# Summing the exponentials of some head pairs on GpSimd before they reach TensorE

## The chip, the core and the metric

The kernel runs on one core of a Trainium2 chip. A core has five engines with instruction queues of their own: PE (TensorE, matrix products, into PSUM), DVE (VectorE, elementwise work), ACT (ScalarE, activation functions and copies), POOL (GpSimd, general cores that also do elementwise work on SBUF) and SP (SyncE, which here issues most DMAs). Each queue is worked through in order, and engines wait for each other by semaphores. The metric is the device time of one execution in microseconds (us). Times of instructions come from one profiled execution.

## What is computed

Two attention layers stand one behind the other, on eight images of 512 channels and 32x32 = 1024 positions. The first is the one that is touched. After a group normalization and the projections it rounds q, k and v to 8 bits over their whole range, and then does plain attention over 8 heads of 64 channels:

```
q, k, v = fake_quant(q), fake_quant(k), fake_quant(v)
w = einsum('bct,bcs->bts', q * scale, k * scale)
w = softmax(w, axis=-1)
a = einsum('bts,bcs->bct', w, v)
x = x + einsum('oc,bct->bot', proj_w, a) + proj_b
```

The softmax needs, for each query, the sum of the exponentials over all 1024 keys. The second layer is single-head attention over 512 channels, with its own normalization and projections, and a residual. All of it is fp32.

## The kernel before

**Stages.** A first stage projects q, k and v of all images and stores them in DRAM, together with their extremes. From then on two streams run through each other: the first layer's attention, and for the image before it the rest (the first layer's output projection, and all of the second layer, whose products are cut up in Strassen's manner into seven, `seven()`).

**Units of the attention.** `attention()` (line 999) walks over 8 images b, 4 pairs of heads j, 2 halves hf of 512 queries, and 8 tiles s of 128 keys: 512 units u, 16 a pair. In a unit `scores(u)` makes two products into a PSUM tile st (128 keys, 2 heads x 512 queries), and ACT writes the exponentials to the fp32 tile pt, 128x1024. There are four slots for pt; the exponential of unit u+4 writes where unit u's was. `split(u)` makes two fp16 parts of pt, in the tile two: a cast, and what the cast left out, a subtraction on DVE. The cast runs on ACT, but for s = 2 and 6 of images 1 to 7 on GpSimd (line 1079). `over_keys` multiplies both parts with v, into av. `totals` sums over keys: both parts times a block of ones, four products a unit, each into its own 32 rows of the PSUM tile sm, over the eight units of a half.

**An iteration** takes four units (lines 1193 to 1237): two scores, then the products with v and the sums of units u to u+3, the splits of two units, two more scores, and after the second iteration of a half `finish`, which copies av and sm out of PSUM on ACT. So scores run six to ten units ahead. Where little other work stands between iterations (`dense`) or after the projection (`late`) the order within an iteration differs.

**The sums' way out.** After the second half, `finish` sends the rows of sums by two small DMAs to a tile apart that has them spread over 128 partitions; there DVE adds the two parts and takes the reciprocal, which goes to DRAM (rs_d) and comes back broadcast over the channels by two DMAs into rs. Later one DVE operation (`divide`) multiplies ao by it.

**Loads.** `load_pair(b, j, u)` (line 942) is called one pair ahead. It fetches raw q, k and v, 128x1024 fp32 each, through a pool of two slots (`raw_p`): q and k at once, and v when q's slot is free. Each takes two DVE passes (`quant`, `quant2`).

**The order.** The second part of the program is planned as it is written: the class `InOrder` keeps a time estimate for DVE, ACT and PE. `do(cost, work, ready)` advances an engine's clock and issues; `later(name, cost, work, ready, within)` puts a chore off, and `fill` issues chores where they fit before the next urgent operation; `settle(name)` issues the rest of a kind. The estimates only set the order of the instructions in the queues; on the chip each instruction waits for its data. GpSimd has no such clock: its instructions stand in program order. Besides the casts and, in the first image, some casts that are done by DMA, it computes the power -1/2 in the group normalizations (line 263).

Of the kernel before, what the change touches and what calls it, by code (L numbers as in the profile page):

```python
# [18 lines left out]
P = 128  # L19
# [39 lines left out]
def attn_pair_kernel(  # L59
# [95 lines left out]
    dve, act, pe = InOrder(nc.vector), InOrder(nc.scalar), InOrder(nc.tensor)  # L155

# [71 lines left out]
    def norm_steps(  # L228
# [22 lines left out]
        def offsets():  # L251
# [11 lines left out]
        nc.gpsimd.tensor_tensor(rstd, rstd, mhalf[:, 0:n], ALU.pow)  # L263
        dve.do(
            0.15, lambda: dve.tensor_mul(rstd, rstd, vec[:, wcol + c0 : wcol + c0 + n]), dve.t + 1.4
# [41 lines left out]
    with ExitStack() as fast:  # L307
# [633 lines left out]

        def load_pair(b, j, u=None):

            nm = f"{b}_{j}"
            raws = []

            def fetch(i, src):
                if (b, j, i) == (0, 0, 2):
                    raw = aop.tile([P, NH, 512], F32, tag="ao", name="raw_first").rearrange(
                        "p h n -> p (h n)"  # L950
                    )
                else:
                    raw = raw_p.tile([P, T], F32, tag="raw", name=f"raw_{nm}_{i}")
# [9 lines left out]
            fetch(1, k_d[b][j])  # L963
# [8 lines left out]
            def quants(i):  # L972
                for n, step in enumerate((quant, quant2, *([whole] if i == 2 and b == 0 else []))):
                    name, work = "qk" if i < 2 else "qv", lambda step=step: step(raws[i], todo[i], i)
                    if u is None or InOrder.planned:
                        dve.later(name, 0.7, work, pe.t + 12.0, 45.0)
# [11 lines left out]
            if (b, j) == (0, 0):  # L988
                fetch(2, v_d[b][:, :, bass.ts(j, P)])
            quants(0)  # L990
            quants(1)
# [7 lines left out]
        def attention():  # L999
# [8 lines left out]
            pts, parts, avs, sms, rss, ready, put_off = {}, {}, {}, {}, {}, {}, {}  # L1008
            st_free, at_hand = [0.0, 0.0], set()
# [3 lines left out]
            def scores(u):  # L1013
# [21 lines left out]
                else:  # L1035
# [3 lines left out]
                    max(pe.t + 0.25, ready.get(u - 4, 0.0) + 0.1),  # L1039
                )  # L1040
                st_free.append(there)
                pts[u] = pt, there

            def split(u):
# [11 lines left out]
                if plain(b, s):  # L1056
                    parts[u], ready[u] = pt, there
                    return
                two = partp.tile([P, 2, 2, 512], F16, tag="two", name=f"two_{b}_{j}_{hf}_{s}")
# [19 lines left out]
                elif s % 4 == 2:  # L1079
                    cast(nc.gpsimd.tensor_copy)  # L1080
# [57 lines left out]
            def finish(b, j, hf, u):  # L1138
# [12 lines left out]
                act.do(0.6, lambda: act.copy(rs[:, hf, :], sms.pop((b, j, hf))))  # L1151
# [6 lines left out]
                for w in range(2):  # L1158
# [10 lines left out]
                def spread():  # L1169
                    r = rcs[:, n * 16 : (n + 1) * 16]  # L1170
                    dve.tensor_add(r, apart[:, 0, :], apart[:, 1, :])
                    dve.reciprocal(r, r)
                    nc.sync.dma_start(rs_d[n].rearrange("r (p k) -> (r p) k", k=16), r)
                    for i, r in enumerate(HALF):
                        nc.sync.dma_start(
                            rs[r], rs_d[n][2 * i : 2 * i + 2, :].partition_broadcast(CH)
                        )
# [15 lines left out]
            for u in range(0, len(units), 4):  # L1193
# [18 lines left out]
                if late:  # L1212
# [700 lines left out]
        dve.t, act.t = pe.t + 4.5, pe.t + 2.0  # L1913
# [372 lines left out]
```

## Time and profile before

| | us |
|---|---|
| median of 3 runs | 2573.52 (2573.21 to 2574.76) |
| profiled execution, its own time | 2572.91 |
| its span, first to last instruction | 2570.9 |
| PE busy | 2522.9 |
| DVE busy | 1897.0 |
| ACT busy | 1347.9 |
| POOL busy | 188.3 |

The attention's first units run from about 590 us on, and its last ones end near 2356 us. From the second to the sixth image one image takes 240.4 us, each alike: the evictions of ao at a pair's end are 64.7, 58.4, 59.7 and 57.5 us apart for the four pairs.

The profile gives, for groups of like instructions, the number, the busy time (overlaps counted once), the mean of one in ns, and the idle time of the engine ahead of them with what ended it. A matrix product of fp32 stands as two records, one of 16 bits as one. Instructions that `InOrder` issues all have line 91, and all products line 209, so they are told apart by their tiles: "two<-pt,two" writes two and reads pt and two. A GpSimd or DVE instruction's time includes what it waits after it has begun. The granted TensorE clock is 0.996 on the mean.

### The profile page before, as it was taken

Reading aid. Unit: us, or ns where it says so; the run is one execution under the profiler, and the core shown is the slowest. Engines: PE = TensorE matmul, PEld = TensorE weight load, DVE = VectorE, ACT = ScalarE, POOL = GpSimd, SP = SyncE. Lnnn points to the kernel's source line nnn. Section 1 sums busy time; section 2 is a strip of 40 time slices with the busy share of each in tenths; the row PEclk is TensorE's granted clock in tenths of the full one; section 3 lists DMA queues with packets and bytes.
Section 4 is the critical chain, followed back from the end, with each engine's and each line's share of the span. In section 5 each row is a group of like instructions: output and inputs, shape, how many; then the busy total and the mean of one; then the engine's idle time right before and its main releaser. Section 6 shows DMA issues by size and latency. Waiting matters only on the chain.

```text
span 2570.9 us, 38729 instructions
## 1 busy us (share of the span) xinstructions
PE 2522.9 (98%) x15670; PEld 1749.2 (68%) x15670; DVE 1897.0 (74%) x2747; ACT 1347.9 (52%) x1685; POOL 188.3 (7%) x167
## 2 busy tenths in 40 slices
PE   7999999999999999999999999999999999999998
PEld 4788888883257756775777577657756775777787
DVE  6788777668887778777777787777778777875544
ACT  3222222218857665665667466746665675664121
POOL 0000000001110001000100100010001000100000
PEclk9999999999999999999999999999999999999999
DMA  4343333336722232123223222322232123212211
GB/s 168 135 146 135 114 117 128 125 130 158 185 83 71 71 115 91 46 79 124 83 68 106 84 87 61 112 101 67 73 114 91 54 71 124 91 47 83 86 38 39
DMA packets 160717, 250.70 MB, mean 98 GB/s; under 512 B 27152, under 2 KB 93712, under 8 KB 159120
## 3 DMA queue, kind: packets, MB, share of 16 engines
q1 hardware_dynamic: 125792, 182.81, 21.8%
q10 hardware_dynamic: 30560, 57.71, 6.5%
q0 software_dynamic: 4176, 7.60, 1.6%
q8 instruction: 125, 2.05, 0.3%
q14 instruction: 64, 0.52, 0.1%
HBM read 153.64 MB, written 86.28 MB: 93 GB/s over the span
## 4 chain that ended last, share of the span: by engine, by line
PE 85%; DVE 4%; issue 3%; ACT 2%; DMA 1%; POOL 0%; ACTq 0%; SPq 0%; DVEq 0%; POOLq 0%
PE s L209 15%; PE o L209 14%; PE qkps L209 12%; PE pj L209 9%; PE av L209 8%; PE v2ps L209 7%; PE g L209 6%; PE vps L209 6%; PE st L209 4%; PE sm L209 3%; DVE two L91 1%; ACT pt L91 1%; DMA two<-spare 1%; DVE acc L91 0%; DVE h L91 0%
## 5 line engine op out<-in xcount | busy, mean ns | idle before, releaser
L91 ACT ACTIVATE pt<-st,esc 128x1024 f32<-128x1024 f32 x467 | 497.0, 1114 | 332.1 <-PE st L209 316.2
L91 DVE TENSOR_TENSOR two<-pt,two 128x1024 f16<-128x1024 f32 x467 | 561.7, 1217 | 133.2 <-POOL two L1073 101.9
L91 ACT CAST two<-pt 128x1024 f16<-128x1024 f32 x346 | 350.8, 1055 | 8.5 <-ACT p L91 5.1
L1073 POOL CAST two<-pt 128x1024 f16<-128x1024 f32 x112 | 148.6, 1326 | 1408.7 <-PE sm L209 736.1
L209 PE MATMUL av<-two,v 128*32 128x512 f16 x3968 | 246.8, 382 | 3.3 <-DVE two L91 2.8
L209 PE MATMUL s<-g,h 128*128 128x256 f32 x1024 | 233.4, 380 | 0.0
L209 PE MATMUL pj<-ao,wp 128*128 128x512 f32 x512 | 223.6, 595 | 0.0
L209 PEld LDWEIGHTS s<-g,h 128*128 128x128 f32 x1024 | 192.9, 190 | 31.0 <-issue 4.3
L91 ACT ACTIVATE u_ring<-qkps,qkbt 128x512 f32<-128x512 f32 x89 | 61.1, 687 | 253.0 <-PE qkps L209 228.5
L209 PEld LDWEIGHTS <-v 128*32 128x32 f16 x3968 | 91.9, 96 | 141.8 <-issue 68.9
L209 PE MATMUL s<-g,sums 128*128 128x256 f32 x768 | 178.5, 381 | 0.2 <-DVE p L91 0.2
L209 PEld LDWEIGHTS pj<-ao,wp 128*128 128x128 f32 x512 | 96.1, 190 | 121.3 <-issue 113.4
L209 PE MATMUL o<-p,v 128*128 128x256 f32 x768 | 175.2, 382 | 1.0 <-DVE p L91 1.0
L209 PE MATMUL st<-q,k 64*128 64x512 bf16 x1024 | 163.7, 383 | 11.6 <-ACT pt L91 7.2
L209 PEld LDWEIGHTS o<-p,v 128*128 128x128 f32 x768 | 144.3, 190 | 27.1 <-issue 5.7
L209 PEld LDWEIGHTS s<-g,sums 128*128 128x128 f32 x768 | 144.6, 190 | 24.5 <-issue 4.6
L209 PE MATMUL sm<-two,ones 128*32 128x512 f16 x1984 | 136.5, 380 | 0.0
L209 PE MATMUL qkps<-half,w_low 128*128 128x512 f32 x480 | 131.9, 397 | 2.0 <-DVE half L91 2.0
L209 PE MATMUL qkps<-half,w_high 128*128 128x512 f32 x480 | 133.8, 401 | 0.0
L209 PE MATMUL qkps<-half,w_mix 128*128 128x512 f32 x480 | 132.3, 398 | 0.4 <-DVE half L91 0.4
L209 PEld LDWEIGHTS <-k 64*128 64x128 bf16 x1024 | 34.7, 94 | 143.7 <-issue 141.6
L209 PE MATMUL v2ps<-wm,h 128*128 128x256 f32 x512 | 119.9, 383 | 1.9 <-ACT g L91 1.3
(226 smaller groups left out, 3906.4 us busy)
## 6 DMA issues: line engine op xcount, KB each, us to landing
rs<-rs_d SPq DMA_DIRECT2D x76, 256.0 KB
x<-in_x_dram SPq DMA_DIRECT2D x32, 512.0 KB
q_d<-wa SPq DMA_DIRECT2D x32, 512.0 KB
k_d<-wa SPq DMA_DIRECT2D x32, 512.0 KB
v_d<-v_ring SPq DMA_DIRECT2D x32, 512.0 KB
raw<-q_d SPq DMA_DIRECT2D x32, 512.0 KB
raw<-k_d SPq DMA_DIRECT2D x32, 512.0 KB
x_d<-h SPq DMA_DIRECT2D x64, 256.0 KB
```

The lines of the kernel that those rows point to most:

```text
L91: ins = self.latest = op(*args, **kw).ins
L209: ins = nc.tensor.matmul(ps, lhsT=lhsT, rhs=rhs, **kw).ins
L1073: copy(two[:, 0], pt)
```

## The change

For units from the second pair of the second image on (u >= SUMMED = 80), and of these for the second and fourth pair (j in BY_SUM = 1, 3):

- `sum_up` adds the eight fp32 tiles pt of a half on GpSimd, in seven adds of 128x1024, into one tile that holds the running sum; the first adds units 0 and 1. It is called from `split`. If the sum of the half before hasn't been read yet, the first add of a half is put off until `total` has been issued.
- `total` replaces `totals`: four fp32 products with ones, of 256 columns each, one for each quarter of the 1024 columns, once a half, before the last four units' products with v.
- The sums then lie as 4 rows of 256 columns a half. They go to apart by one DMA instead of two, need no add, and come back by four DMAs of half the width instead of two.
- An exponential waits for the add of the unit four before it, too.

For all units from 80 on, in all four pairs: the casts that were GpSimd's are ACT's. The tile of the running sum takes one of the two slots of `raw_p`; q, k and v of a pair, from those on that are loaded at u >= 80, share the other and are fetched one after another, each when the one before has been quantized, with the planner's lead of 7 us in place of 12.

GpSimd gets a clock and an order of its own (`pool`), and the normalization's power goes through it.

```diff
@@ -153,6 +153,7 @@
...
     dve, act, pe = InOrder(nc.vector), InOrder(nc.scalar), InOrder(nc.tensor)
+    pool = InOrder(nc.gpsimd)
...
@@ -260,9 +261,11 @@
...
         dve.do(0.15, lambda: dve.tensor_scalar(rstd, ps2, EPS, None, ALU.add))
-        nc.gpsimd.tensor_tensor(rstd, rstd, mhalf[:, 0:n], ALU.pow)
+        there = pool.do(
+            1.3, lambda: pool.tensor_tensor(rstd, rstd, mhalf[:, 0:n], ALU.pow), dve.t + 0.1
+        )
         dve.do(
-            0.15, lambda: dve.tensor_mul(rstd, rstd, vec[:, wcol + c0 : wcol + c0 + n]), dve.t + 1.4
+            0.15, lambda: dve.tensor_mul(rstd, rstd, vec[:, wcol + c0 : wcol + c0 + n]), there
         )
...
@@ -939,16 +942,25 @@
...
+        SUMMED = (PAIRS + 1) * NH * NT
+        BY_SUM = (1, 3)
+        rooms = {}
+
         def load_pair(b, j, u=None):
...
             raws = []
+            one_room = u is not None and u >= SUMMED
+            if one_room and "raw" not in rooms:
+                rooms["raw"] = raw_p.tile([P, T], F32, tag="raw", name="raw_room")
...
                     )
+                elif one_room:
+                    raw = rooms["raw"]
                 else:
...
@@ -960,7 +972,8 @@
...
             fetch(0, q_d[b][j])
-            fetch(1, k_d[b][j])
+            if not one_room:
+                fetch(1, k_d[b][j])
             qt = qkp.tile([P, T], BF, tag="q", name=f"q_{nm}")
...
@@ -973,7 +986,7 @@
...
                     if u is None or InOrder.planned:
-                        dve.later(name, 0.7, work, pe.t + 12.0, 45.0)
+                        dve.later(name, 0.7, work, pe.t + (7.0 if one_room else 12.0), 45.0)
                     else:
...
@@ -987,7 +1000,15 @@
...
                 fetch(2, v_d[b][:, :, bass.ts(j, P)])
+            def fetch_k():
+                fetch(1, k_d[b][j])
+                quants(1)
+                dve.later("qk", 0.0, fetch_v)
+
             quants(0)
+            if one_room:
+                dve.later("qk", 0.0, fetch_k)
+                return qt, kt, vt
             quants(1)
...
@@ -1006,6 +1027,7 @@
...
             pts, parts, avs, sms, rss, ready, put_off = {}, {}, {}, {}, {}, {}, {}
+            added = {}
             st_free, at_hand = [0.0, 0.0], set()
@@ -1036,10 +1058,54 @@
...
                     1.12, lambda: act.activation(pt, st, AF.Exp, scale=esc),
-                    max(pe.t + 0.25, ready.get(u - 4, 0.0) + 0.1),
+                    max(pe.t + 0.25, max(ready.get(u - 4, 0.0), added.get(u - 4, 0.0)) + 0.1),
                 )
...
                 pts[u] = pt, there
+
+            def summed(u):
+                return u >= SUMMED and units[u][1] in BY_SUM
+
+            def sum_up(u, pt, there):
+
+                s = units[u][-1]
+                if "sum" not in rooms:
+                    rooms["sum"] = raw_p.tile([P, T], F32, tag="raw", name="sum_room")
+                if s == 0:
+                    rooms["first"] = pt
+                    return
+                acc = rooms["sum"]
+                src = rooms["first"].rearrange("p i n -> p (i n)") if s == 1 else acc
+
+                def add():
+                    added[u] = pool.do(
+                        2.2, lambda: pool.tensor_tensor(
+                            acc, src, pt.rearrange("p i n -> p (i n)"), ALU.add
+                        ), there + 0.1,
+                    )
+                    if s == 1:
+                        added[u - 1] = added[u]
+
+                if s == 1 and rooms.get("busy"):
+                    rooms["next"] = add
+                else:
+                    add()
+                    rooms["busy"] = True
+
+            def total(b, j, hf, u):
+
+                awaits(added[u + 3])
+                pe.t += 0.12
+                sms[b, j, hf] = sm = av_bank(f"sm_{b}_{j}_{hf}")[:, 0:256]
+                for n in range(4):
+                    mm(
+                        sm[n * QUAD : (n + 1) * QUAD, :], lhsT=ones[:, 0:QUAD],
+                        rhs=rooms["sum"][:, n * 256 : (n + 1) * 256], start=True, stop=True,
+                    )
+                rooms["busy"] = "next" in rooms
+                if "next" in rooms:
+                    pool.t = max(pool.t, pe.t + 0.25)
+                    rooms.pop("next")()
...
@@ -1056,6 +1122,8 @@
...
                     return
+                if summed(u):
+                    sum_up(u, pt, there)
                 two = partp.tile([P, 2, 2, 512], F16, tag="two", name=f"two_{b}_{j}_{hf}_{s}")
...
@@ -1076,8 +1144,8 @@
...
                     cast(dve.tensor_copy if s in CAST_BY_DVE else act.copy)
-                elif s % 4 == 2:
-                    cast(nc.gpsimd.tensor_copy)
+                elif u < SUMMED and s % 4 == 2:
+                    cast(pool.tensor_copy)
                 elif not InOrder.planned and s == 5:
...
@@ -1148,14 +1216,22 @@
...
                 act.do(0.6, lambda: act.copy(aot[:, hf, :], avs.pop((b, j, hf))))
-                act.do(0.6, lambda: act.copy(rs[:, hf, :], sms.pop((b, j, hf))))
+                sm = sms.pop((b, j, hf))
+                whole, flat = summed(u), rs.rearrange("p h n -> p (h n)")
+                k = sm.shape[-1]
+                act.do(0.6, lambda: act.copy(flat[:, hf * k : (hf + 1) * k], sm))
                 if hf == 0:
...
                 apart = small.tile([P, 2, 16], F32, tag="apart", name=f"apart_{nm}")
-                for w in range(2):
+                if whole:
+                    nc.sync.dma_start(
+                        apart[:, 0, :],
+                        flat[0:P:QUAD, 0:512].rearrange("r (p k) -> r p k", k=16),
+                    )
+                for w in range(0 if whole else 2):
                     nc.sync.dma_start(
...
@@ -1168,13 +1244,22 @@
...
                     r = rcs[:, n * 16 : (n + 1) * 16]
-                    dve.tensor_add(r, apart[:, 0, :], apart[:, 1, :])
-                    dve.reciprocal(r, r)
+                    if whole:
+                        dve.reciprocal(r, apart[:, 0, :])
+                    else:
+                        dve.tensor_add(r, apart[:, 0, :], apart[:, 1, :])
+                        dve.reciprocal(r, r)
                     nc.sync.dma_start(rs_d[n].rearrange("r (p k) -> (r p) k", k=16), r)
                     for i, r in enumerate(HALF):
-                        nc.sync.dma_start(
-                            rs[r], rs_d[n][2 * i : 2 * i + 2, :].partition_broadcast(CH)
-                        )
+                        src = rs_d[n][2 * i : 2 * i + 2, :]
+                        if whole:
+                            for a in range(2):
+                                nc.sync.dma_start(
+                                    rs[r, :, a * 256 : (a + 1) * 256],
+                                    src[a].rearrange("(h c) -> h c", h=NH).partition_broadcast(CH),
+                                )
+                        else:
+                            nc.sync.dma_start(rs[r], src.partition_broadcast(CH))
                     if InOrder.planned:
...
@@ -1209,7 +1294,18 @@
...
                     two(scores, u + 6)
-                if late:
+                if summed(u):
+                    if late:
+                        over_keys((u, u + 1))
+                        two(scores, u + 6)
+                    if s == NT - 4:
+                        total(b, j, hf, u)
+                    over_keys(range(u + 2 * late, u + 4))
+                    for v in range(u, u + 4):
+                        del parts[v]
+                    two(split, u + 6)
+                    two(scores, u + 8)
+                elif late:
                     over_keys((u, u + 1))
...
@@ -1910,7 +2006,7 @@
...
         tc.add_manual_dep(warm.ins, dve.last.name, IN_ORDER, reason="order")
-        dve.t, act.t = pe.t + 4.5, pe.t + 2.0
+        dve.t, act.t, pool.t = pe.t + 4.5, pe.t + 2.0, pe.t + 7.0
         InOrder.planned = True
...
```

## The prediction

> **What bounds the kernel now.** I read four views, in this order: the page (which engine is full, what the last chain is made of), the stretches of one middle image cut by head pair, the chain inside such a stretch, and the timeline where GpSimd and VectorE meet. The page first:
>
> ```profile
> PE 2522.9 (98%) x15670; PEld 1749.2 (68%) x15670; DVE 1897.0 (74%) x2747; ACT 1347.9 (52%) x1685; POOL 188.3 (7%) x167
> ...
> PE 85%; DVE 4%; issue 3%; ACT 2%; DMA 1%; POOL 0%; ACTq 0%; SPq 0%; DVEq 0%; POOLq 0%
> ...
> L91 DVE TENSOR_TENSOR two<-pt,two 128x1024 f16<-128x1024 f32 x467 | 561.7, 1217 | 133.2 <-POOL two L1073 101.9
> L1073 POOL CAST two<-pt 128x1024 f16<-128x1024 f32 x112 | 148.6, 1326 | 1408.7 <-PE sm L209 736.1
> L209 PE MATMUL sm<-two,ones 128*32 128x512 f16 x1984 | 136.5, 380 | 0.0
> ```
>
> TensorE carries the chain; the sums over keys (sm) are part of it, and GpSimd is nearly empty. That is the case for the change. The next view decides against it. It gives engine busy times for the image whose pairs end at 1462.9, 1521.3, 1581.0 and 1638.6 us (its evictions of ao), cut at the first exponentials of each pair: second, third, fourth, and the next image's first.
>
> ```profile
> 1443.00:1501.70 58.70, 58.60 (x356) 37.77 (x352) 46.39 (x72) 31.72 (x40) 7.60 (x4) 1.00 0.29 99
> 1501.70:1561.00 59.30, 59.30 (x429) 43.35 (x427) 43.50 (x49) 41.48 (x52) 4.96 (x4) 1.00 0.19 59
> 1561.00:1619.80 58.80, 58.80 (x446) 42.36 (x448) 45.85 (x58) 37.83 (x50) 4.86 (x4) 1.00 0.27 78
> 1619.80:1683.50 63.70, 62.59 (x440) 38.27 (x432) 47.15 (x57) 40.51 (x50) 5.95 (x5) 1.00 0.33 109
> ```
>
> Columns: window, length, then busy time of PE, weight load, DVE, ACT, POOL. PE is full in every pair; DVE has 12 to 16 us free a pair. Two shorter windows inside the first of these, one iteration (four key tiles) each, show that its free time is not spread evenly: here DVE, the third pair of numbers, is already full.
>
> ```profile
> 1472.40:1487.00 14.60, 14.60 (x106) 10.38 (x104) 14.57 (x21) 9.58 (x13) 3.42 (x1) 1.00 0.39 132
> 1487.00:1501.70 14.70, 14.60 (x106) 10.38 (x104) 14.63 (x22) 10.53 (x14) 1.22 (x1) 1.00 0.30 100
> ```
>
> The timeline shows what happens when GpSimd reads SBUF beside DVE.
>
> ```profile
> 1233.86 2.35 DVE L91 TENSOR_TENSOR two<-pt,two 128x1024 f16<-128x1024 f32 x2
> ...
> 1234.58 3.12 POOL L1073 CAST two<-pt 128x1024 f16<-128x1024 f32 x1 [3.39 <-PE sm L209]
> ...
> 1236.12 0.68 DVE L91 TENSOR_TENSOR sums<-h 128x512 f32<-128x512 f32 x1
> ...
> 1236.84 1.41 DVE L91 TENSOR_TENSOR sums<-h,sums 128x512 f32<-128x512 f32 x1
> ```
>
> The cast, 1.04 us when alone (1219.44), stood for 3.12 us until the DVE operations before it were through; then the DVE subtraction, 0.68 us alone, took 1.41 because the cast was running. The same pattern repeats in other rows: raw<-raw,rcp takes 0.735 to 1.529 us, acc<-acc,p 0.68 to 1.41, and the tiny GpSimd power of the normalization 1.92 behind a DVE subtraction against 1.01 in the first stage. So a GpSimd read and a DVE operation with two SBUF inputs, or a fast fp32 tensor-scalar, exclude each other, edges apart.
>
> **The change, part by part.** The affected pairs are the second and fourth of images 1 to 7: 14 pairs, 28 halves.
>
> TensorE, removed. The chain of the second pair and the timeline around the first image's fp32 sums:
>
> ```profile
> 1474.44 0.86 PE sm L209 x16
> ...
> 1503.69 0.86 PE sm L209 x16
> ```
>
> ```profile
> 642.94 1.03 PE L209 MATMUL sm<-aside,ones 128*32 128x512 f32 x8
> 643.90 0.60 PE L209 MATMUL st<-q,k 64*128 64x512 bf16 x4
> ```
>
> A half has two such blocks of sums: 1.72 us (two blocks with their change of layout 1.94). Added: four fp32 products of 256 columns. Four of 512 columns took 0.96 to the next start, 0.86 without the change of layout; half of it is 0.43, and 0.53 with it. Net 1.2 a half, between 1.2 and 1.5; I take 1.2. Over 28 halves that is 33 us, all on the path today.
>
> GpSimd, added: seven fp32 adds of 128x1024 a half, 196 in all. No row has one. Below, the lone cast, 1.04 us, which reads one such operand; above, two of these, 2.08, since an add reads two. I take 2.1, near the upper end, because the number of operands read is what differs. The page "GPSIMD Engine Reference", section 3.1, has 4.50 us for 2048 elements: an estimate of 2.25 from it would raise the surplus below by 4 us an image. Fourteen adds are 29 us a pair.
>
> VectorE, the price of those adds. I sum, in the DVE groups of these windows, the rows that have two SBUF inputs or are fast tensor-scalars (two, raw, q, k, v, acc, x, ao, sums, h, g<-g, p, vsum), overlaps counted once: 35 us in the second pair, 41 in the fourth, 156 of 240.5 in the image. The casts leave GpSimd, which returns about 1.3 us a pair of blocked time (the raw row's mean is 0.87 against 0.745 alone). So the shared reading way needs 35+29-1.3 = 63 us in the second pair, where there are 58.7, and 41+29-1.3 = 69 in the fourth, where there are 58.8: 4 and 10 over, 14 an image. Over a whole image it would fit (156+59 = 215 of 240). The rows also show where this count is too high: the 1.04 us cast delayed the subtraction by 0.73 (1.41 less 0.68), so some 0.3 us at the edges of the two overlap. Fourteen adds with such edges block 4 us less a pair: 6 over an image instead of 14. I take 8.5, nearer to 6, because that row has the same two engines meeting; 8.5 by seven images is 59 us. The page "SBUF — State Buffer" of the Trainium skill, section "SBUF: two separate sides", says instead that the one that starts first keeps the shared way for its whole instruction and the other blocks fully. By that rule the surplus would be the 14, 98 us in all; the row's overlap speaks for less.
>
> Can such lateness be carried into the pair behind, where DVE has 15.8 and 16.5 us free? The subtractions behind the exponentials have most of an iteration, 14.6 us. But the evictions from PSUM (g<-g,vsum, v<-v2ps, p<-s) stand in the same in-order queue, two banks deep, with products of about 1.8 us on TensorE: late by more than one product less their own 0.69 us, they stop it at once, and seven or eight adds fall into the two full iterations above. So I let nothing be carried in the likeliest case. As these pairs are then not paced by TensorE, the 33 are not subtracted again.
>
> ScalarE: 108 casts (112 less four) move onto it, 1.055 each, 4.2 us a pair. It is busy 32 to 41 of 59 us; the cover is its idle time ahead of the exponentials (309 us from 800 to 2400 us). If the cover were gone, its PSUM copies would be late: bound 0 to 1 us a pair; I take 0. DVE's waits for GpSimd's casts (102 us in all) go; what is late next there is PE, so nothing is gained.
>
> Slots: an exponential now waits for the add of four tiles before. Behind it on ACT stand PSUM copies. In a second half the first add waits for the total of the half before; it starts some 3 us ahead of the exponential that needs its slot, and takes 2.1, so nothing unless DVE holds it: 0 to 2 us for 14 halves; taken inside the 59.
>
> POOL's order: the power of the normalization now queues behind adds and can be 2 to 4 us late (bound 0 to 28 us over seven); DVE waits for it in order, and the next products with h. Its time falls into the same busy second pair; not added twice.
>
> Loads and SP: q, k and v of a pair go one after another through one slot. A stage is the issue (0.33 to 0.56), the planned 7 us and two passes of 0.75: about 9, so k is there 18 us after the start, where the scores have two iterations, 29 us; v has the whole pair. K's and v's issues wait on SP for DVE's second pass, with the sums' small transfers queued behind; before, the same issues waited for the same slot. Two more issues of rs a pair (0.52 each) and one less of apart (0.55): hidden, the division being due 20 us later. On ACT the copy of sums shrinks, on DVE one 0.175 us add goes: 14 times each, hidden.
>
> Sum: 2572.9 (profiled execution; span 2570.9 and 2 around it; the median is 2573.5) plus 59 gives 2632.
>
> **Rivals.** *It fits* (faster): the lateness is carried, TensorE stays the bound and the 33 us come out: 2540, or 2560 if half is lost. For it: the image as a whole has room, and 1408.7 us of idle GpSimd. Against: full DVE iterations. It turns on the time of one add: with 5 us carried a pair, the second pair holds at 56.3+5 >= 33.7+14t, t up to 1.9, the fourth at 39.7+14t, t up to 1.5. An add under about 1.5 us makes this the case. *GpSimd starves* (slower): back-to-back DVE operations hold the way, as in the 3.12 us cast, each add takes 2.1+2.1, 3.5 of them an iteration make 14.7 against some 14, and the exponentials wait for slots: 0.7 to 2.5 us over 56 iterations, 2612 to 2713. *The gain is eaten*: loads in a row, or the power, late by 1 to 2 us a pair over 23 pairs, 23 to 46 against the 33: 2563 to 2586.
>
> **How the numbers follow.** Port over-full in its two pairs 0.50 (own range 2580 to 2671, the last with no overlap at the edges, 98 us); starved 0.16; fits 0.27; eaten 0.07. The range goes from just under the full gain, 2537, to the starved end, 2713. Within 0.2%, about what a measurement of this kernel tells from no change (2568.4 to 2578.7), lie most of the last case and edges of its neighbours: 0.05; faster 0.28, slower 0.67.
>
> **What would show it.** Right: adds of 2.1 us and more with long stretched ones; DVE rows with two SBUF inputs up in pairs two and four, PE rows there waiting for DVE, those pairs above 58.5 us, pairs one and three unchanged; sm rows down by 896 instructions. Wrong: adds near 1.5 us or DVE rows unchanged, PE still 99% full, and pairs shorter by 2.4 us each; or the waits standing at raw loads or ACT's casts.

## The result, and the profile after

The changed kernel takes 2892.82 us (median of 4 runs, 2888.04 to 2898.23) where the kernel before takes 2573.36: a ratio of 1.1249, with a 95% interval of 1.1222 to 1.1276. It is slower, as forecast, but by 319 us where 59 were forecast, far above the top of the range (2713).

The page of the changed kernel, by the same rows as before (engine totals, granted clock by slices, the last chain by engine, the groups concerned):

```profile
PE 2589.9 (90%) x14998; PEld 1786.6 (62%) x14998; DVE 2159.8 (75%) x2733; ACT 1449.5 (50%) x1793; POOL 574.3 (20%) x255
...
PEclk9999999999999999998999899989998999899999
...
PE 53%; DVE 30%; issue 4%; ACT 4%; DMA 4%; POOL 1%; SPq 0%; ACTq 0%; DVEq 0%; POOLq 0%
...
L91 DVE TENSOR_TENSOR two<-pt,two 128x1024 f16<-128x1024 f32 x467 | 623.0, 1362 | 112.7 <-ACT two L91 111.7
L91 POOL TENSOR_TENSOR sum_room<-sum_room,pt 128x1024 f32<-128x1024 f32 x168 | 446.8, 2660 | 417.1 <-ACT pt L91 407.7
...
L91 POOL TENSOR_TENSOR sum_room<-pt,pt 128x1024 f32<-128x1024 f32 x28 | 83.1, 2969 | 949.5 <-ACT pt L91 794.4
```

Three things are to be seen. VectorE (DVE) is no fuller as a share, 75%, but its busy time is up by 263 us although it has 14 instructions less: it is its own waiting that counts as busy. Its part of the last chain went from 4% to 30%. And TensorE (PE) is busy for 67 us longer with 672 records less; the row of the clock, all nines before, has an eight every few slices.

The stretches of a middle image, cut as before at the first exponentials of the pairs: second, third, fourth, and the next image's first (length, then busy time of PE, weight load, DVE, ACT, POOL; then the granted clock).

```profile
1582.00:1662.60 80.60, 64.03 (x371) 42.13 (x369) 71.46 (x78) 35.09 (x43) 37.68 (x14) 0.89 0.24 79
1662.60:1727.60 65.00, 60.77 (x416) 44.23 (x416) 44.56 (x48) 46.21 (x57) 2.77 (x1) 0.97 0.15 46
1727.60:1801.10 73.50, 59.54 (x371) 42.37 (x372) 58.86 (x54) 39.54 (x51) 30.47 (x12) 0.91 0.20 62
1801.10:1869.50 68.40, 64.12 (x401) 38.52 (x400) 46.04 (x53) 45.78 (x55) 5.87 (x3) 1.00 0.32 101
```

The image takes 287.5 us where it took 240.5: 21.9 more in the second pair, 5.7 in the third, 14.7 in the fourth, 4.7 in the first. PE now stands idle for 16.6 and 14.0 us in the two pairs with adds (0.1 and 0 before). But no engine is full there: DVE is busy for 71.5 of 80.6 us and 58.9 of 73.5, and GpSimd (POOL) for less than half.

How that comes about is in the timeline of the second pair. DVE, POOL and PE rows of the second half (x and idle time in brackets as before; adjacent like instructions are one row):

```profile
1629.59 2.77 POOL L91 TENSOR_TENSOR sum_room<-pt,pt 128x1024 f32<-128x1024 f32 x1 [10.29 <-PE sm L210]
...
1632.44 11.48 POOL L91 TENSOR_TENSOR sum_room<-sum_room,pt 128x1024 f32<-128x1024 f32 x4
1633.37 2.84 DVE L91 TENSOR_TENSOR sums<-h 128x512 f32<-128x512 f32 x1
...
1636.24 2.74 DVE L91 TENSOR_TENSOR sums<-h,sums 128x512 f32<-128x512 f32 x1
...
1638.90 2.83 DVE L91 TENSOR_TENSOR kept_u<-kept_u,rs 128x512 f32<-128x512 f32 x1
1641.77 2.84 DVE L91 SCALAR_TENSOR_TENSOR x<-kept_u,ob,x 128x256 f32<-128x256 f32 x2
...
1647.78 0.68 DVE L91 TENSOR_TENSOR v<-v2ps,kept_u 128x512 f32<-128x512 f32 x1
...
1648.52 3.78 PE L210 MATMUL v2ps<-wm,sums 128*128 128x256 f32 x8 [8.60 <-DVE v L91]
...
1656.34 6.08 POOL L91 TENSOR_TENSOR sum_room<-sum_room,pt 128x1024 f32<-128x1024 f32 x2 [12.41 <-ACT pt L91]
```

While four adds run back to back (11.48 us), DVE gets one instruction through for each add: operations of 0.68 us stand for 2.7 to 2.8. They go strictly by turns. Everything behind them in DVE's queue is late, in the end the eviction v<-v2ps. It takes its normal 0.68 us, POOL being idle by then, but it stands last in the row: PE has waited 8.60 us for it. Then the picture turns over: DVE catches up with POOL idle, since PE's pause made the scores and so the exponentials late, and the next add has waited 12.41 us for one of them.

The window view of four overlapping pieces of that stretch gives the clock beside it: the adds, PE's pause, the 10.2 us of the half clock, and the products after the pause.

```profile
1632.44:1643.92 11.48, 6.58 (x30) 5.13 (x28) 11.41 (x5) 6.98 (x10) 11.24 (x4) 0.97 0.00 0
1639.91:1648.52 8.61, 0.01 (x2) 0.01 (x1) 8.54 (x10) 1.53 (x2) 3.94 (x2) 0.69 0.11 36
1643.10:1653.34 10.24, 4.82 (x11) 3.87 (x12) 9.40 (x13) 2.11 (x3) 0.83 (x1) 0.51 0.23 78
1648.52:1655.14 6.62, 6.62 (x22) 4.80 (x22) 4.38 (x6) 0.64 (x2) 0.00 (x0) 0.63 0.22 74
```

The clock falls to half during the pause and stays there for some 5 us after PE has work again: the eight products v2ps<-wm,sums take 3.78 us, the eight just before the pause 1.89.

From 800 to 2700 us the view of waits names the same places (engine waiting, what for: us in total, times, longest):

```profile
ACT pt L91 <- DVE two L91: 165.6, 67, 5.7
...
PE v2ps L210 <- DVE v L91: 55.4, 12, 8.6
...
PE av L210 <- DVE two L91: 44.4, 25, 5.7
...
ACT pt L91 <- POOL sum_room L91: 28.9, 13, 3.5
```

Exponentials wait for a slot of pt because DVE's subtraction is late, nearly six times as long as because an add is late.

### The profile page after: what moved, and what is told of

Read it like the earlier page. It is cut to its first block, busy times and chain, and to the rows that moved or that the text cites. A ratio compares the mean times of both kernels' runs of the same rounds, so it can differ in the third digit from the quotient of the medians.

```text
span 2886.3 us, 37713 instructions
## 1 busy us (share of the span) xinstructions
PE 2589.9 (90%) x14998; PEld 1786.6 (62%) x14998; DVE 2159.8 (75%) x2733; ACT 1449.5 (50%) x1793; POOL 574.3 (20%) x255
## 4 chain that ended last, share of the span: by engine, by line
PE 53%; DVE 30%; issue 4%; ACT 4%; DMA 4%; POOL 1%; SPq 0%; ACTq 0%; DVEq 0%; POOLq 0%
PE s L210 12%; DVE two L91 11%; PE qkps L210 11%; PE vps L210 5%; PE v2ps L210 5%; PE pj L210 5%; PE o L210 4%; PE g L210 3%; DVE g L91 3%; PE av L210 3%; DVE x L91 3%; DVE kept_u L91 2%; DVE h L91 2%; DMA rs<-rs_d 2%; PE st L210 2%
## 5 line engine op out<-in xcount | busy, mean ns | idle before, releaser
L91 DVE TENSOR_TENSOR two<-pt,two 128x1024 f16<-128x1024 f32 x467 | 623.0, 1362 | 112.7 <-ACT two L91 111.7
L91 POOL TENSOR_TENSOR sum_room<-sum_room,pt 128x1024 f32<-128x1024 f32 x168 | 446.8, 2660 | 417.1 <-ACT pt L91 407.7
L91 ACT CAST two<-pt 128x1024 f16<-128x1024 f32 x454 | 457.5, 1055 | 45.7 <-issue 31.9
L91 POOL TENSOR_TENSOR sum_room<-pt,pt 128x1024 f32<-128x1024 f32 x28 | 83.1, 2969 | 949.5 <-ACT pt L91 794.4
L210 PE MATMUL s<-g,sums 128*128 128x256 f32 x768 | 195.2, 407 | 36.7 <-DVE g L91 35.5
L210 PEld LDWEIGHTS s<-g,sums 128*128 128x128 f32 x768 | 154.9, 205 | 68.4 <-issue 42.6
L210 PE MATMUL v2ps<-wm,h 128*128 128x256 f32 x512 | 130.7, 408 | 33.5 <-DVE v L91 17.1
L210 PEld LDWEIGHTS v2ps<-wm,h 128*128 128x128 f32 x512 | 102.2, 204 | 58.2 <-DVE v L91 19.6
L210 PE MATMUL v2ps<-wm,sums 128*128 128x256 f32 x384 | 103.8, 424 | 38.3 <-DVE v L91 38.2
L210 PE MATMUL g<-sums,wa 128*128 128x256 f32 x384 | 103.1, 421 | 35.0 <-ACT kept_u L91 31.7
```

What stands on the lines that cost most here:

```text
L91: ins = self.latest = op(*args, **kw).ins
L210: ins = nc.tensor.matmul(ps, lhsT=lhsT, rhs=rhs, **kw).ins
```

## The experiments

The theory after this reading (*held up*): GpSimd's adds hold VectorE up by a good part of their length, VectorE's free time in a pair does not absorb that, and TensorE stands and loses its clock. The rivals: the added waits and the rearranged loads and casts do it without the adds (*moves*); or GpSimd's writes or its mere activity do it, not its reading (*writes*). The runs below that leave the adds out take the sums from a constant.

### The changed kernel without its adds

```diff
                     rooms["sum"] = raw_p.tile([P, T], F32, tag="raw", name="sum_room")
+                    nc.gpsimd.memset(rooms["sum"], 40.0)
...
-                        2.2, lambda: pool.tensor_tensor(
-                            acc, src, pt.rearrange("p i n -> p (i n)"), ALU.add
-                        ), there + 0.1,
+                        2.2, lambda: None, there + 0.1,
```

> The changed kernel with the 196 adds on GpSimd left out: the tile of the running sum is filled with 40 once, so the softmax sums are a constant and the sum over keys is not computed. The order of all other instructions is as in the changed kernel, with the casts on ScalarE and the loads through one slot. Theory 1 (the adds keep VectorE's operations with two SBUF inputs waiting, and the rest follows): TensorE is the bound again and its 33 us come out, 2535 to 2560 us. Rival 2 (the casts moved to ScalarE, or the loads one after another, are what is late): 2800 us or more. Rival 3 (both halves matter): between, 2620 to 2780.

Measured: 2598.75 us, ratio to the kernel before 1.0115 (1.0098 to 1.0132): above the 2535 to 2560 of theory 1, and under both rivals (2620 and more). The instructions of PE, DVE and ACT stand in the same order as with the adds. From its page:

```profile
PE 2497.2 (96%) x14998; PEld 1737.5 (67%) x14998; DVE 1850.9 (71%) x2733; ACT 1453.2 (56%) x1793; POOL 44.7 (2%) x60
...
PEclk9999999999999999999999999999999999999999
...
L91 DVE TENSOR_TENSOR two<-pt,two 128x1024 f16<-128x1024 f32 x467 | 553.5, 1216 | 93.4 <-ACT two L91 91.9
```

So 294 of the 319 us are the adds (292 by the spans). Taking the adds alone away brings 309 us of DVE busy time back (2159.8 to 1850.9). PE's pauses over 0.4 us, added up from 700 us on, fall from 252.7 us to 55.5, and the time at half clock, from 720 us to PE's last product, from 221.9 us to 3.4. These two make the difference of the spans: 197 us of idle PE, and at most 109 (half of 218.5) for the clock, 306 at most against 292.4. The run takes away the waits for the adds too (slots, totals); of these the exponentials' are the 28.9 us above, and the run with fills below keeps waits of this kind without the loss. And the rest is not free either: without the adds the kernel is still 29 us over the kernel before (2569.9 beside it), though TensorE has less to do.

### Where the rest goes: TensorE's part, the casts, the loads

First TensorE's part of the change alone: the new sums, taken from a constant, with the casts on GpSimd and the loads as before. Then that with the casts on ScalarE (ACT), and that with the loads in a row.

```diff
-            one_room = u is not None and u >= SUMMED
+            one_room = False
...
-                elif u < SUMMED and s % 4 == 2:
+                elif s % 4 == 2:
                     cast(pool.tensor_copy)
```

(The first two lines are undone in the run with the loads, the last two in the run with the casts. In all three the adds are left out and the sum is a product of two constants, of the same size.)

> TensorE's part of the change alone: four fp32 products of 256 columns a half in place of the sums, of constants, so that the sums over keys are not computed; no adds on GpSimd, the casts back on GpSimd and the loads through two slots as before the change. Theory: 28 halves at 1.2 us, 2540 us (2530 to 2550). With e1 it prices the moved casts and the loads in a row: under 10 us between the two if they are hidden.

> TensorE's part alone (as before, with constant sums), and the 108 casts moved from GpSimd to ScalarE. TensorE's part alone ran in 2545 us and the changed kernel without adds in 2599: 54 us lie with the casts or with the loads in a row. If the casts: 2585 to 2600. If the loads: 2540 to 2555. If both: about 2570.

> TensorE's part alone (with constant sums), and the loads of q, k and v one after another through one slot, the casts on GpSimd. If the loads are what costs: 2585 to 2600. If the casts: 2540 to 2555. If both: about 2570.

| run | us | ratio (95%) |
|---|---|---|
| TensorE's part alone | 2544.77 | 0.9901 (0.9884 to 0.9917) |
| and the casts on ACT | 2587.99 | 1.0065 (1.0049 to 1.0082) |
| and the loads in a row | 2559.30 | 0.9951 (0.9934 to 0.9967) |

TensorE's part gains 25 us. The casts cost 43, as the expectation for the casts had it; the loads 14.5, between what was expected if only the casts cost and if both did. 2545 + 43 + 14.5 is 2602.5, and the changed kernel without adds took 2598.75. Nothing large is left. The waits of the run with the casts, and below it of that with the loads, both over the middle images:

```profile
DVE two L91 <- ACT two L91: 92.9, 51, 5.5
...
PE av L210 <- DVE two L91: 13.4, 12, 1.5
```

```profile
PE st L210 <- DVE k L91: 10.3, 6, 1.8
```

Before, DVE's subtraction two waited 95.7 us for GpSimd's casts and 21.7 for ACT's. With all casts on ACT these waits didn't go: they are for ACT now, and part of them reaches PE. PE's waits over the middle images are 48 us against 12 in the run with TensorE's part alone; 20 of them are of the products av for the two parts of pt (13.4 for DVE, 6.2 for ACT), the rest is spread over other products. The pair with the projection, the first, went from 64.7 us to between 67.7 and 68.8; the third is 1.5 us longer than in that run, the second 1.1 to 3.0. With the loads in a row the scores of a pair wait up to 1.8 us for k, once an image; the second pair takes 1.3 to 2.9 us longer than in the run with TensorE's part alone.

### What of an add does the harm: reading or writing

Each add is made small, and two fills of the sum tile stand behind it, together about as long.

```diff
+            def writes(acc, src, new):
+                pool.tensor_tensor(acc[:, 0:2], src[:, 0:2], new[:, 0:2], ALU.add)
+                pool.memset(acc[:, 2:T], 40.0)
+                pool.memset(acc[:, 2:T], 40.0)
...
-                        2.2, lambda: pool.tensor_tensor(
-                            acc, src, pt.rearrange("p i n -> p (i n)"), ALU.add
-                        ), there + 0.1,
+                        2.2, lambda: writes(acc, src, pt.rearrange("p i n -> p (i n)")), there + 0.1,
```

> The changed kernel with each add of 1024 columns replaced by an add of two columns and two memsets of the other 1022 columns, so that GpSimd works as often and about as long but reads next to nothing; the sums over keys are not computed for those columns. If it is GpSimd's reading beside VectorE's second SBUF input that costs: VectorE's subtractions back at 1.22 us, 2535 to 2620 us (what is left falls on the fast tensor-scalars). If any work of GpSimd's, or its place in the order, costs as much: 2800 to 2900 us.

Measured: 2610.15 us, 1.0154 (1.0129 to 1.0178): within the range for reading, and 11 us more than without adds, though POOL is busy for 504.0 us. The groups, with different shapes kept apart:

```profile
L91 DVE TENSOR_TENSOR two<-pt,two 128x1024 f16<-128x1024 f32 x467 | 553.0, 1215 | 94.9 <-ACT two L91 93.2 <-POOL two L91 1.4
L91 POOL MEMSET sum_room<- 128x1022 f32 x392 | 386.7, 987 | 11.3
...
L91 DVE SCALAR_TENSOR_TENSOR x<-kept_u,ob,x 128x256 f32<-128x256 f32 x128 | 55.0, 476 | 1.4
L91 DVE TENSOR_SCALAR q<-raw_room,bhi 128x1024 bf16<-128x1024 f32 x26 | 28.5, 1095 | 0.4
```

DVE operations with two SBUF inputs (two, x) stand at their times without any adds, 1216 and 476 ns. A fast tensor-scalar (q) does not: 1095 ns against 751. So what holds the two-input operations is GpSimd's reading; its writing holds only the tensor-scalars. The rival *writes* has at most 11 us.

The Trainium skill's page "SBUF — State Buffer", section "SBUF: two separate sides", says that VectorE and GpSimd lock a shared pair of ports for a whole instruction, VectorE for its fast modes, or for two SBUF inputs if GpSimd reads. The runs agree: the alternation above, and these rows of who is held by what; only the edges of two such instructions overlap a little (some 0.2 us, see below).

### The length of an add

Half the work, and the whole work in four pieces.

```diff
-                            acc, src, pt.rearrange("p i n -> p (i n)"), ALU.add
+                            acc[:, 0:512], src[:, 0:512],
+                            pt.rearrange("p i n -> p (i n)")[:, 0:512], ALU.add
```

```diff
+            def quarters_of(acc, src, new):
+                for n in range(4):
+                    c = bass.ts(n, 256)
+                    pool.tensor_tensor(acc[:, c], src[:, c], new[:, c], ALU.add)
```

(The first leaves out the upper half of the columns; the sums are taken from the lower half twice.)

> The changed kernel with adds of 512 columns instead of 1024, the sums of the first 512 columns used for both heads, so that half of the sums over keys is left out. An add should take about 1.2 us. Theory 1, with the loss in proportion to the time that an add holds VectorE up: about half of the 350 us between the changed kernel and the one without adds, 2680 to 2750 us. If short adds fit between VectorE's operations, as the prediction's case of 1.5 us had it: 2540 to 2600 us. If the number of adds counts and not their length: 2850 us.

> The changed kernel, whole, with each add of 1024 columns made as four adds of 256: the same work, and the same sums. By VectorE's busy time the halved adds (1.27 us alone) each held VectorE up for 0.53 us and the whole ones (2.35) for 1.58, both 0.75 less than their length. If 0.75 us of every add is hidden, whatever its length, a quarter of some 0.7 us is hidden altogether: 2600 to 2680. If the time that GpSimd reads counts in sum, however it is cut: 2860 to 2950.

Measured: 2687.76 us, 1.0456 (1.0435 to 1.0476), within theory 1's range, and 2775.05 us, 1.0792 (1.0771 to 1.0814). The second lies between the two expectations and decides for neither: an add doesn't have a fixed part that is hidden, as I had read from the first two lengths, and cutting it up doesn't let DVE through at no cost. But the two runs are worth having for another reading. I take DVE's busy time above that of the kernel without adds as the time that it was held up, and set it against the span. The totals of the halves, then of the quarters:

```profile
PE 2529.2 (94%) x14998; PEld 1752.1 (65%) x14998; DVE 1955.0 (73%) x2733; ACT 1452.4 (54%) x1793; POOL 347.7 (13%) x255
```

```profile
PE 2558.9 (92%) x14998; PEld 1766.0 (64%) x14998; DVE 2057.0 (74%) x2733; ACT 1449.5 (52%) x1793; POOL 838.9 (30%) x843
```

| adds | alone, us | DVE held up, us | span longer, us | ratio of the two |
|---|---|---|---|---|
| whole, 196 | 2.34 | 309 (1.58 an add) | 292 | 0.95 |
| in quarters, 784 | 0.71 | 206 (0.26 an add) | 181 | 0.88 |
| halves, 196 | 1.26 | 104 (0.53 an add) | 91 | 0.88 |

(Alone: the quickest of a kind. Spans and busy times are those of the profiled executions.) Whatever their length, for each microsecond in which GpSimd held VectorE up the span grew by some 0.9, on an engine that was free for a quarter of the time. Two things make up these 0.9. PE's pauses (over 0.4 us, as above) grew by 197, 116 and 57 us, which is 0.64, 0.56 and 0.55 of the time that DVE was held up; the half clock after them adds at most 109, 55 and 27 us. Whole adds hold DVE for two thirds of their length, quarters for 37%; why shorter pieces hold it less was not tried.

### The same adds on VectorE

If DVE's free time is usable by work that is put where it is free, adds done by DVE itself should be cheaper than adds that hold it up.

```diff
-                def add():
-                    added[u] = pool.do(
-                        2.2, lambda: pool.tensor_tensor(
...
+                def work():
+                    dve.tensor_tensor(acc, src, pt.rearrange("p i n -> p (i n)"), ALU.add)
+                    added[u] = dve.t
...
+                def add():
+                    dve.later("add", elements(1024), work, there + 0.1, 9.0)
...
                     if n < B * PAIRS:
+                        settle("qv")
```

(With a call that issues the put-off add when an exponential or the total needs it, and with a pair's last quantizations issued before the next pair's loads.)

> The changed kernel, whole, with the 196 adds done by VectorE itself as planned chores instead of by GpSimd. VectorE does such a subtraction in 1.22 us, so this is 239 us of work for it; GpSimd's adds lengthened VectorE's own busy time by 309 us (2160 against 1851 without adds). Theory 1: VectorE is better off doing the work than being kept waiting: 2700 to 2800 us, under the 2893 of the changed kernel. If GpSimd does take work off VectorE's path, however slowly: over 2893.

Measured: 2698.37 us, 1.0495 (1.0465 to 1.0526), just under the lower end of theory 1: 194 us less than on GpSimd, with all the work done. The groups:

```profile
L91 DVE TENSOR_TENSOR two<-pt,two 128x1024 f16<-128x1024 f32 x467 | 551.2, 1215 | 81.8 <-ACT two L91 81.3 <-POOL two L91 0.2
L91 DVE TENSOR_TENSOR sum_room<-sum_room,pt 128x1024 f32<-128x1024 f32 x168 | 204.5, 1217 | 3.5
```

An add is 1.22 us on DVE and lengthens nothing else. DVE's busy time rises by 220 us (to 2071.1) and the span by 103: 0.47 of it, half of what the held-up time cost. PE's pauses grew by 63 us, 0.28 of it, where the waits gave 0.64. So most of the work that was placed by plan was absorbed, and about a third of the waits that fall where they will, before the clock's loss. (The quantizations that were moved ahead are in this run too, and not separated.) The page "GPSIMD Engine Reference", section 4.1, advises VectorE for elementwise work; here that is worth 194 us, though neither place makes the change pay.

### One pair alone

```diff
-        BY_SUM = (1, 3)
+        BY_SUM = (1,)
```

> The change for the second pair alone (with casts on ScalarE and loads in a row for all pairs, as in the changed kernel). Without adds 2599, with both pairs 2893: 294 us for two pairs. The prediction had the second pair over-full by 4 us and the fourth by 10 an image. If that count tells where the time goes: the second alone costs 80 to 120, 2680 to 2720. If what counts is that VectorE is already full through two iterations of the second pair: 150 to 190, 2750 to 2790.

> The change for the fourth pair alone (the rest as in the changed kernel). By the prediction's count it is the dearer one: 170 to 210 above the 2599 without adds, 2770 to 2810. By VectorE's full iterations, which lie in the second: 100 to 140, 2700 to 2740.

With the second pair alone 2753.40 us, 1.0709 (1.0669 to 1.0749); with the fourth alone (BY_SUM = (3,)) 2747.15, 1.0685 (1.0654 to 1.0716). The first is what VectorE's full iterations gave, the second is between the two counts: neither count holds for both. The casts and loads of all pairs are as in the changed kernel in both. For one pair the kernel without adds would stand near 2611, by an estimate: the 2598.75 with no adds in either, plus half of TensorE's 25 us, which only one of the pairs now brings. Above that the second pair's adds cost 142 us and the fourth's 136, together 278 of the 294. The two pairs cost alike, and separately.

### The casts back on GpSimd, with the adds

```diff
-                elif u < SUMMED and s % 4 == 2:
+                elif s % 4 == 2:
```

> The changed kernel, whole, with the casts of the third and seventh key tiles back on GpSimd. Without adds, casts on ScalarE cost 43 us. If that price stands beside the adds: 2850. If the casts' reading (104 times 1.04 us) adds to the adds' on the way that VectorE shares: about 2893 or above, up to 2950.

Measured: 2872.64 us, 1.1173 (1.1141 to 1.1205), between the two expectations and 20 us less than the change. Without adds the same step is worth 43. What takes the difference was not separated; beside the adds DVE waits 135.1 us for GpSimd's casts (101.9 before the change), and its busy time is 31 us longer than with the change. The first and third pairs (64.8 and 60.2 us in the fifth image) are as before the change again; the second and fourth, 78.9 and 79.6, hold all of the loss.

### Fewer sums without adds

The change's aim, fewer products for the sums, in another way: from the second image on the sums are taken from the fp16 casts alone, two units to a product's place. The low parts of the exponentials are left out of the sums (not of the products with v).

```diff
             def totals(us):
                 pe.t += 0.12
+                if units[us[0]][0] > 0:
+                    for u in us[::2]:
...
+                        for n in range(4):
+                            mm(sms[b, j, hf][n * QUAD : (n + 1) * QUAD, :], lhsT=ones16,
+                               rhs=parts[u + n // 2][:, 0, n % 2, :], start=(s == 0),
+                               stop=(s == NT - 2))
```

> The kernel before, with another way to make TensorE's sums cheaper, without any work on another engine: for images 1 to 7 the sums are taken of the fp16 casts alone, without the parts that the casts leave out, and two units share one product of 32-row blocks, so eight products an iteration in place of 16. This leaves the low parts out of the sums (not out of the products with v). If TensorE paces all of it, 112 iterations at 0.43 us come out: 48 us, 2522 us. If shortened iterations bring another engine to the fore as in the run of TensorE's part alone, where 25 of 36 came: 2530 to 2545. If nothing: 2570.

Measured: 2539.84 us, 0.9873 (0.9857 to 0.9890), 1.3% under the kernel before and within the middle expectation. It takes out 896 of the records sm<-two,ones, as many as the change does, touches no other engine, and leaves VectorE where it was (1892.8 us). TensorE's busy time falls by 44 us, of which 31 come out.

## Why the prediction was wrong in size

*TensorE's gain.* Taken as 1.2 us a half and 33 in all. Without adds the old block of sums is 1.73 us a half and the new products 0.46 (predicted 1.72 and 0.53): 1.27 a half, 36 over 28. PE's busy time did fall by 36 (2522.9 to 2487.1); 25 to 28 came out of the end. A size slightly off. That "the 33 are not subtracted again" was right for the changed kernel.

*The time of an add.* Taken as 2.1 us from two lone casts; alone it is 2.34, and 2.66 to 2.97 on the mean with its own waiting. The estimate of 2.25 from the skill's page was the nearer one. It makes the pair's adds 33 us rather than 29, 47 us in all: a smaller part of the miss.

*Who excludes whom.* Right, with corrections. The rows with two SBUF inputs rose: over the middle images, without adds and with them, g<-g takes 687 and 1382 ns, x 475 and 934, sums<-h,sums 689 and 1703, kept_u<-kept_u,rs 680 and 1219; the last was left out of the count of 35 and 41 us. p<-s,kept_u, which was in that count, has one input in PSUM and is not held: five of these ran wholly inside an add and took 691 ns each, as always (688 on the mean). The eviction v<-v2ps did not rise either (691 and 687), but only one of 34 met an add (678 ns). And the edges overlap a little less than the 0.3 us read from the cast: in the timeline above the subtraction ahead of the four adds ends at 1633.44 and the last add at 1643.92; in these 10.48 us stand three DVE operations of 0.68 too, which leaves 2.11 an add, 0.23 less than alone. The 8.5 us taken for an image stood for adds of some 1.9.

*The failed step* is the sum after it: "So the shared reading way needs 35+29-1.3 = 63 us in the second pair, where there are 58.7", 4 and 10 over, with 8.5 an image taken. This compares what a whole pair needs with what a whole pair has, and so spends all of DVE's free time on the waits before it counts any loss. I had written that nothing can be carried into the next pair, and that full iterations of DVE exist within a pair; yet the sum lets lateness be carried freely inside the pair. The runs show in its place that a wait imposed on DVE lengthens the span by about 0.9 of its length: 22 us of hold-up a pair (309 over 14), 21 us a pair lost (294 over 14). Of the 309, 197 stand as longer pauses of PE; at most 109 us of lost clock are the rest. DVE's queue is in order, and the late instruction stands ahead of evictions with which PE has at most a few us of slack; PE's pause then makes the exponentials late, so POOL idles while DVE catches up. The free time is mostly spent after the loss, not in place of it. The same error gave the fourth pair more than twice the second's loss, 10 against 4; they cost 136 and 142. A better price of the add doesn't save the sum: with the 2.11 us that adds take by turns it gives 4.5 and 10.4 over, some 105 us, near the 98 of the full-lock rule. The mechanism was right; PE's pauses alone grew by 197 us.

*The clock* was in no step. A pause of PE was priced at its length; on top come at most 109 us, over a third of the adds' cost, because the clock halves after many pauses of about 2 us and more (last section).

*ScalarE's casts*, taken at 0 with a bound of 0 to 1 us a pair (27 at most): 43 measured. The cover named, ACT's idle time ahead of the exponentials, is largest in the pair with the projection, 23.0 of 64.7 us before; but the casts didn't use it there. With them it is 24.6 us, and the pair is 3.5 us longer. That DVE's waits for GpSimd's casts go was wrong: they became waits for ACT's casts.

*The loads in a row*, called hidden: 14.5, k being up to 1.8 us late. Casts and loads together, 58, exceed TensorE's gain without any add, so the rival "the gain is eaten" was priced too low (23 to 46) and not on the casts; by itself it makes the kernel 1.2% longer than before.

*Slots.* Right: an exponential waits for an add 28.9 us in all in the part shown, little beside the rest. "GpSimd starves" is not what happened: adds are up to 4.64 us long, but 2.66 on the mean, and it is DVE's lateness that exponentials wait for.

*POOL's power behind the adds.* Priced at 0 to 28 us and not tried by itself, but the trace answers it. In the six images from 1000 to 2500 us POOL had stood idle for 2.53 us when the power began, 0.08 us after the DVE operation that feeds it. It took 1.93 us (1.92 before), and DVE waited 0.91 us for it (0.90 before). It was never behind an add, and cost nothing.

*What would show it.* Adds of 2.1 us and more, DVE rows up, PE waiting for DVE, those pairs above 58.5 us: all there. "Pairs one and three unchanged" failed: 67.9 against 64.7 us and 65.0 against 59.7, by the evictions of ao in the fifth image. The first is the casts' (67.9 without adds). Of the third's 5.3 us the casts have 1.5 (61.2 without adds); the rest goes with the fourth pair's adds, the first of which run before the third pair's last eviction: the third pair takes 61.2 with the second pair's adds alone and 63.3 to 65.0 with the fourth's. The sm rows are down by the 896 named.

## What to carry to other kernels

An engine that is busy for three quarters of the time and feeds the full one in order has no store of free time that waits can be charged to: count a wait that another engine forces on it at nearly its whole length (0.9 here), and only work that can be placed in its gaps at about half; in both numbers the clock's loss is included, and without it they are 0.6 and 0.3 here. Compare needs and room over the distance by which a queue may be late (here a few us, two PSUM banks), not over a stage. Price what a change moves, the casts and loads here, before what it saves: they ate the gain before the adds began.

## What was not expected of the hardware

*The clock gives way to pauses well under 3.4 us.* In the changed kernel the trace has 45 stretches at half clock between 720 us and PE's last product, 27 of 3.4 us, 16 of 6.8 and 2 of 10.2. PE's idle time in the 3.42 us ahead of each, added up from pauses over 0.3 us, is 1.92 us or more in all 45, and fully 3.4 in only nine. With adds in quarters it is 1.86 or more in 24 of 25, and 1.30 in one. Pauses with no half clock are nearly all under 1.9 us, but a few of 2.9 us, and with quarters of 3.1 and 3.5, had none, so the phase seems to matter; this was only read off, not tried. The skill's page "TensorE: Matmul & The Clock Gate", part 1, has the half clock after at least one idle window of about 3.4 us: the length of the stretches agrees with such windows, but less than a whole idle one was enough here.

*GpSimd's times by length.* The quickest fp32 adds of two SBUF tiles took 0.71 us for 128x256, 1.26 for 128x512 and 2.34 for 128x1024: by these about 0.17 us and 2.1 ns for each element of a partition. VectorE's took 1.22 for the last.

*Tiny operations suffer whole adds.* DVE's rcs<-apart, 128x16, takes 176 ns without adds and 1157 with them on the mean over the middle images, and gd_b<-gd_b, 128x4, 162 and 1582: the wait is set by the other engine's instruction, not by one's own size.
